# Layer 1's mixture of experts on pairs sorted by expert

## The chip, the cores and the metric

One Trainium2 chip; the kernel runs on one of its cores. The metric is the device time of one execution in microseconds, as the median over runs. A core has a matrix engine (TensorE, PE in the profile; its weight loads are PEld), VectorE (DVE), ScalarE (ACT), GpSimd (POOL) and SyncE (SP), each with its own queue that is worked off in order, and 16 DMA engines that all of them share.

## The reference

Two layers over `x` of 4 sequences, 1024 tokens, 128 features, all fp32. Each layer computes `x = x + s * silu(f)`, where `s` is an attention and `f` a mixture of experts, both of the layer-normed `x`. Layer 0 has 16 heads of 8 with relative positions, and one of 8 experts per token. Layer 1 has a causal differential attention (8 heads from 16 score maps, normed by head), and this mixture:

```python
logits = x @ router_w.T                       # T x 8
topk_logits, topk_idx = top_k(logits, 2)
probs = softmax(topk_logits)
combine[t, topk_idx] += probs                 # T x 8, two entries per row
hmid = gelu(einsum('th,efh->etf', x, w1) + b1)   # 8 experts, F = 256
y = einsum('etf,ehf->eth', hmid, w2) + b2
out = einsum('eth,te->th', y, combine)
```

Only two of the eight experts enter a token's result.

## The kernel before

Each layer and sequence is a `Sequence` `q` (`q.b` its number, `seqs` the eight in order: layer 0's four, then layer 1's four). Its attention is cut into steps (a group of 4 score maps, 256 queries) and these into slots, one block of 128 keys each: 128 slots for a sequence of layer 0, 80 for one of layer 1 (causal). `q.first` and `q.last` are its first slot and the slot after its last.

The order of all instructions is written out by hand. A loop goes over the slots; in each it issues the transposed scores (`turned_scores`, L912, into PSUM tag `st`, two buffers, exponentials on ACT at L950), half of the row-maximum searches (L793 scores, L853 maxima on DVE), the weighting of the slot before (`weigh`, L959), the other half, and then what `at(slot, f)` or, inside such work, `after(n, f)` has put there. `spread_over(lo, hi, work)` places work evenly over free slots. The searches of a step are done 7 slots or more before it in layer 1; the maxima go through `spread_maxima` and a store (`qs<-mt`) into the query tile. SP issues nearly all DMAs, in this written order: queries (`load_queries`, 10 slots before their first search), keys (`load_keys`), the splits of Q and K into bf16 pieces.

Around the change: `layernorm` makes `xn`, `transpose_xn` its transpose `xnT`; `values_of` also gives the router's logits; `route` finds the two largest of them, their softmax weights `p1`, `p2`, and the combine matrix `q.w`; `turn_route` and `expert_bias` start the gate's sum `q.g` with `b2`. Layer 1's experts are dense: for each half of the tokens and each of the 8 experts, `hidden` (L635, L643) makes 256 hidden values for 512 tokens with two 512-column matmuls and two Gelus, four experts in a row in one slot, and `experts1` (L655, L663, L670) multiplies back, weights by a column of `q.w` on DVE, and adds to `q.g` on POOL:

```python
for half in range(2):
    for e0 in range(0, NE, 4):
        some = range(e0, e0 + 4)
        work.append((lambda h=half, s=some: [hidden(q, h, e) for e in s], False))
        work += [(lambda h=half, e=e: experts1(q, h, e), True) for e in some]
```

The expert weights are transposed during layer 0 (`turn_expert`), stored to DRAM, and loaded at layer 1's first slot by `expert_tables` into the two `pos` tiles, which layer 0 needs no longer. `gate` applies tanh and two products to `q.g`; `norm_heads`, `turn_o` and `output` end a sequence.

## Time and profile before

| what | value |
|---|---|
| median of 3 runs | 2171.2 us (2167.64 to 2174.56) |
| the profiled execution | 2145.35 us, span 2143.6 us, granted clock 0.978 |
| layer 0, then layer 1 (first slot at about 1226 us) | 1226 us, 917 us |
| one sequence of layer 1 | 222 to 225 us |
| PE, DVE, ACT, POOL busy from 1226 to 2143 us | 839.07, 634.86, 430.26, 234.84 us |

The busy time of an engine is the time in which it worked on an instruction of the program; matmuls are pipelined, their ends are modelled, and a busy PE need not be at its peak. In the lists of groups a line names the source line, engine, operation, what is written and read, the shapes and the count; then come the busy time and the mean duration in ns, and after the second bar the engine's idle time just before these instructions and what ended it. The granted clock is the share of TensorE's full clock that the chip let through.

### The profile page before, as it was taken

The numbers are of one execution on the slowest core, as the hardware profiler recorded it, in microseconds if no ns is written. First come the engines' busy times: TensorE is split into PE (matmuls) and PEld (weight loads), VectorE is DVE, ScalarE is ACT, GpSimd is POOL, SyncE is SP. The second block draws the span as 40 slices with busy tenths as digits, with TensorE's granted clock in tenths as the row PEclk, the third lists the DMA queues.
The fourth block names the chain that finished last, engine by engine and source line by source line (L and its number), as shares of the span: only waits on it lengthen the run. The fifth ranks groups of instructions, "written<-read, shape, count | busy, mean of one in ns | idle before, by whom it ended". The sixth has DMA issues, their size and how long they took to land.

```text
span 2143.6 us, 45507 instructions
## 1 busy us (share of the span) xinstructions
PE 1969.8 (92%) x17424; PEld 1125.9 (53%) x17424; DVE 1613.7 (75%) x4197; ACT 1327.8 (62%) x1801; POOL 585.8 (27%) x907
## 2 busy tenths in 40 slices
PE   4899999999999999999999989999999899999996
PEld 2455555555555555555555445555556555555553
DVE  4788888787887888887888867778666876686563
ACT  1577778777778777886777544444555444544542
POOL 3013332224321333221323113313231324131112
PEclk9999999999999999998999989999999999999996
DMA  4766776767777767775767111201120212111001
GB/s 137 242 194 205 223 229 204 222 207 214 216 217 227 205 215 225 215 226 186 207 205 234 59 44 31 63 22 55 33 61 24 54 33 63 22 39 40 21 4 32
DMA packets 232975, 286.98 MB, mean 134 GB/s; under 512 B 14932, under 2 KB 206972, under 8 KB 232492
## 3 DMA queue, kind: packets, MB, share of 16 engines
q1 hardware_dynamic: 228272, 282.38, 44.1%
q8 instruction: 139, 2.28, 0.4%
q10 hardware_dynamic: 4476, 1.60, 0.3%
q14 instruction: 88, 0.72, 0.1%
HBM read 153.28 MB, written 129.76 MB: 132 GB/s over the span
## 4 chain that ended last, share of the span: by engine, by line
PE 63%; DVE 25%; DMA 7%; issue 3%; POOL 1%; SPq 1%; ACT 0%; DVEq 0%; ACTq 0%; POOLq 0%
PE s L793 14%; PE o L959 14%; DVE mx L853 7%; PE st L912 7%; PE st L944 6%; PE bank L655 6%; PE hid_ps L635 5%; DVE sp L809 4%; DMA qs<-qd 3%; DVE m L885 3%; DVE mx L828 2%; PE bank L600 2%; PE bank L716 2%; DVE mrest L887 2%; DMA skew<-rows 1%
## 5 line engine op out<-in xcount | busy, mean ns | idle before, releaser
L950 ACT ACTIVATE eT<-st 128x1024 f32<-128x1024 f32 x832 | 822.8, 991 | 561.5 <-PE st L912 515.7
L793 PE MATMUL s<-ksl,qs 72*128 72x384 bf16 (+3 forms) x1984 | 532.6, 312 | 64.1 <-DVE mx L853 35.9
L959 PE MATMUL o<-eT,va 128*9 128x256 f32 (+2 forms) x6656 | 520.8, 380 | 1.7 <-ACT eT L950 1.3
L853 DVE TENSOR_REDUCE mx<-s 128x1 f32<-128x512 f32 (+3 forms) x608 | 395.4, 657 | 55.3 <-PE s L832 26.4
L828 DVE TENSOR_REDUCE mx<-s 128x1 f32<-128x512 f32 x512 | 352.2, 688 | 106.6 <-PE s L793 101.1
L809 DVE CUSTOM_DVE_ANT_0 sp<-s,pos 128x512 f32<-128x512 f32 x512 | 352.2, 688 | 78.5 <-PE s L793 42.5
L793 PEld LDWEIGHTS <-qs 72*128 72x128 bf16 x2496 | 206.4, 98 | 382.7 <-issue 363.1
L878 ACT ACTIVATE sp<-sp,nm 128x384 f32<-128x384 f32 (+1 forms) x512 | 297.8, 583 | 107.7 <-DVE nm L870 107.7
L912 PE MATMUL st<-qs,ksl 75*128 75x256 bf16 (+1 forms) x2304 | 329.4, 253 | 0.0
L912 PEld LDWEIGHTS <-ksl 75*128 75x128 bf16 x2304 | 215.2, 99 | 70.6 <-issue 33.5
L944 PE MATMUL st<-ident,sp 128*128 128x128 f32 x1408 | 214.0, 277 | 0.2
L959 PEld LDWEIGHTS o<-eT,va 128*9 128x9 f32 (+1 forms) x6656 | 112.4, 91 | 182.5 <-issue 126.1
L732 POOL COPY rows<-rows 128x512 f32<-128x512 f32 x128 | 78.3, 612 | 428.5 <-ACT rows L723 391.7
L670 POOL TENSOR_TENSOR g<-g,part 128x512 f32<-128x512 f32 x64 | 81.2, 1269 | 402.8 <-DVE part L663 334.7
L944 PEld LDWEIGHTS st<-ident,sp 128*128 128x128 f32 x1408 | 172.6, 143 | 25.4 <-issue 15.5
L663 DVE TENSOR_TENSOR part<-bank,r1hot 128x512 f32<-128x512 f32 x64 | 44.2, 691 | 174.3 <-PE bank L655 159.8
L723 ACT COPY rows<-bank 128x512 f32<-128x512 f32 x256 | 147.8, 577 | 33.5 <-PE bank L716 22.2
L793 PE MATMUL s<-ksr,qs 72*128 72x128 bf16 (+3 forms) x512 | 157.3, 308 | 6.1 <-DVE mx L828 4.7
L655 PEld LDWEIGHTS bank<-pos,hid 128*128 128x128 f32 x1024 | 126.8, 198 | 15.3 <-issue 11.9
L655 PE MATMUL bank<-pos,hid 128*128 128x128 f32 x1024 | 131.2, 283 | 0.0
L716 PE MATMUL bank<-fs,qs 72*128 72x256 bf16 x512 | 101.2, 280 | 31.3 <-ACT rows L723 9.1
L912 PE MATMUL st<-qs,ksr 75*128 75x256 bf16 (+1 forms) x768 | 122.8, 260 | 0.0
(209 smaller groups left out, 2182.4 us busy)
## 6 DMA issues: line engine op xcount, KB each, us to landing
skew<-rows SPq DMA_DIRECT2D x128, 768.0 KB
pos<-skew SPq DMA_DIRECT2D x96, 768.0 KB
qs<-qd SPq DMA_DIRECT2D x384, 48.0 KB
ksl<-kd SPq DMA_DIRECT2D x96, 192.0 KB
pos<-skew SPq DMA_DIRECT2D x32, 512.0 KB
kd<-piece SPq DMA_DIRECT2D x36, 256.0 KB
ksr<-kd SPq DMA_DIRECT2D x48, 192.0 KB
qd<-piece SPq DMA_DIRECT2D x35, 256.0 KB
```

The lines of the kernel that those rows point to most:

```text
L655: nc.tensor.matmul(ps[:, m * P : (m + 1) * P], lhsT=h[:, c, m * P : (m + 1) * P], rhs=w2t[:, 2 * e + c, :], start=(c == 0), stop=(c == 1),)
L716: nc.tensor.matmul(ps[:, j * 256 : (j + 1) * 256], lhsT=st.qs[:NS, 2 * k + j, m * P : (m + 1) * P], rhs=fs, start=True, stop=True,)
L723: nc.scalar.copy(rows[:, 2 * k : 2 * k + 2, 0:256], ps.rearrange("p (m v) -> p m v", v=256))
L793: nc.tensor.matmul(ps, lhsT=st.qs[:NS, j, m * P : (m + 1) * P], rhs=keys[:NS, j, lo * P : hi * P], start=start, stop=stop,)
L809: nc.vector.tensor_tensor_reduce(out=st.sp[m][:, j * BW : j * BW + 512], in0=ps, in1=st.pos[m][:, j, :], scale=1.0, scalar=-FMAX, op0=ALU.add,
L828: nc.vector.tensor_reduce(largest(st)[:, m, j, 1:2], ps, AX.X, ALU.max)
L853: nc.vector.tensor_reduce(largest(st)[:, m, heads[0] : heads[-1] + 1, slot], parts, AX.X, ALU.max,)
L878: nc.scalar.activation(cols, cols, AF.Identity, bias=st.nm[:, m, j : j + 1])
L912: nc.tensor.matmul(ps[:, j, lo * P : hi * P], lhsT=keys[side][:, j, jb * P : (jb + 1) * P], rhs=st.qs[:, j, lo * P : hi * P], start=start, ...
L944: nc.tensor.transpose(ps[:, j, m * P : (m + 1) * P], st.sp[m][:, at : at + P], ident)
L950: nc.scalar.activation(eT[:, :, skip:], ps[:, :, skip:], AF.Exp)
L959: nc.tensor.matmul(o_ps[32 * j : 32 * j + va.shape[-1], skip : 2 * P], lhsT=va, rhs=eT[:, j, skip:], start=(jb == st.blocks[0]), stop=(jb ...
```

## The change

Each token of layer 1 makes two pairs (token, expert). The pairs are put in order of expert, each expert's padded to tiles of 128 rows: at most 23 tiles (`PT`) where the dense form has 64 products of 128 tokens with an expert. `pair_rows` counts with small matmuls and finds each pair's row and each tile's expert. `sort_tokens` scatters the normed tokens, read back from a DRAM copy (`xnd`), to their rows in `xsd`, 16 indirect DMAs of 128 rows from POOL's queue; `load_weights` gathers a tile's weights and bias, one indirect DMA a tile, from a table with 514 values a row; `load_pairs` and `turn_pairs` load and transpose four tiles; `hidden` and `results` work on four tiles, each with its own expert's weights, and the results go to `ysd`; `pick` gathers them back per token, 16 indirect DMAs, and DVE adds them to `q.g` with their weight. The weights and picks lie in the `pos` tiles and in the right-side key tiles, which layer 1 doesn't use. The next sequence's norm, values and routing are moved to earlier slots, and some steps of the norms a slot or more back. The output layout, layer 0's experts and the attention's arithmetic stay.

```diff
+PT = 2 * NT + NE - 1
+TRASH = PT * P
+WR = 4 * P + 2
...
+    onesb = const.tile([P, P], BF16, tag="onesb", name="onesb")
+    nc.gpsimd.memset(onesb, 1.0)
+    before = const.tile([P, P], BF16, tag="before", name="before")
+    up_to = const.tile([P, NE, NE], F32, tag="up_to", name="up_to")
...
-    w1d = dconst.tile([P, 2 * NE, P], F32, tag="w1d", name="w1d")
-    w2d = dconst.tile([P, 2 * NE, P], F32, tag="w2d", name="w2d")
+    wd = dconst.tile([NE * P, WR], F32, tag="wd", name="wd")
...
-            nc.sync.dma_start(w1d[:, 2 * e : 2 * e + 2, :], t[:, 0:2, :])
-            nc.sync.dma_start(w2d[:, 2 * e : 2 * e + 2, :], t[:, 2:4, :])
+            nc.sync.dma_start(wd[e * P : (e + 1) * P, : 4 * P], t.rearrange("p m f -> p (m f)"))
...
+    xnd = [dconst.tile([S, P], F32, tag=f"xnd{m}", name=f"xnd{m}") for m in range(2)]
+    xsd = [dconst.tile([TRASH + P, P], F32, tag=f"xsd{m}", name=f"xsd{m}") for m in range(2)]
+    ysd = [dconst.tile([TRASH + P, P], F32, tag=f"ysd{m}", name=f"ysd{m}") for m in range(2)]
+    spare = [t.rearrange("p h v -> p (h v)") for t in pos_tiles]
+    spare += [stacks[m][1].rearrange("p h t -> p (h t)").bitcast(F32) for m in range(2)]
+    weight_tiles = [t[:, m * WR : (m + 1) * WR] for m in range(3) for t in spare]
+    picked_tiles = [
+        t[:, 3 * WR + m * P : 3 * WR + (m + 1) * P] for m in range(3) for t in spare
+    ]
...
+    def zero_pairs():
+        zero = pos_tiles[0][:, 0:1, BW:].to_broadcast([P, PT + 1, P])
+        for t in xsd:
+            nc.scalar.dma_start(t.rearrange("(n p) d -> p n d", p=P), zero)
+        for t in ysd:
+            nc.scalar.dma_start(t[TRASH:], pos_tiles[0][:, 0, BW:])
...
-        after(1, guess)
-        after(2, refine)
+        after(2, guess)
+        after(3, refine)
...
-        after(10, lambda: nc.vector.tensor_tensor(xn, xn, over(rstd, full), ALU.mult))
+        after(11, lambda: nc.vector.tensor_tensor(xn, xn, over(rstd, full), ALU.mult))
+        if q.layer == 1:
+            q.xnd = xnd[q.b % 2].rearrange("(n p) d -> p n d", p=P)
+            after(12, lambda: nc.sync.dma_start(q.xnd, xn))
...
+                *pair_rows(q, hot1, hot2),
...
-            after(n, f)
+            after(n // 2 if q.layer else n, f)
...
+    def pair_rows(q, hot1, hot2):
+        ...
+        def counted():
+            ps = bank()
+            ahead.append(ps[:, : (NT + 1) * NE].rearrange("p (n e) -> p n e", e=NE))
+            nc.tensor.matmul(
+                ps[:, : (NT + 1) * NE],
+                lhsT=before,
+                rhs=both.rearrange("p n e -> p (n e)"),
+                start=True,
+                stop=False,
+            )
+            for n in range(NT):
+                nc.tensor.matmul(
+                    ahead[0][:, n + 1 :, :],
+                    lhsT=onesb,
+                    rhs=both[:, n : n + 1, :].to_broadcast([P, NT - n, NE]),
+                    start=False,
+                    stop=(n == NT - 1),
+                )
+            nc.vector.tensor_scalar(tiles, ahead[0][:, NT, :], P - 1.0, None, ALU.add)
+            nc.vector.tensor_copy(row, ahead[0][:, :NT, :])
+        many = [P, PT, NE]
+        work = [
+            lambda: nc.vector.memset(both[:, NT, :], 0.0),
+            lambda: nc.vector.tensor_tensor(both[:, :NT, :], hot1, hot2, ALU.add),
+            counted,
+            ...
+        for hot, rows in zip((hot1, hot2), q.rows):
+            work += [
+                lambda hot=hot: nc.vector.tensor_tensor(prod, hot, row, ALU.mult),
+                lambda: nc.vector.tensor_reduce(sums, prod, AX.X, ALU.add),
+                lambda rows=rows: nc.vector.tensor_scalar(
+                    rows, sums, float(TRASH), None, ALU.add
+                ),
+            ]
+        return work + [
+            lambda: nc.vector.tensor_tensor(
+                where,
+                tiles_at.unsqueeze(2).to_broadcast(many),
+                end.unsqueeze(1).to_broadcast(many),
+                ALU.is_ge,
+            ),
+            lambda: nc.vector.tensor_reduce(which, where, AX.X, ALU.add),
+            lambda: nc.vector.tensor_scalar(which, which, NE - 1.0, float(P), ALU.min, ALU.mult),
+            lambda: nc.vector.tensor_scalar(q.weight_rows, which, own_row, None, ALU.add),
+        ]
...
-    def expert_tables():
-        w1t = pos_tiles[0].rearrange("p h (c f) -> p (h c) f", f=P)
-        w2t = pos_tiles[1].rearrange("p h (c f) -> p (h c) f", f=P)
-        nc.sync.dma_start(w1t, w1d)
-        nc.sync.dma_start(w2t, w2d)
-        return w1t, w2t
-    def hidden(q, half, e):
-        w1t, _ = q.tables
-        ps = ps_t.tile([P, 2, 512], F32, tag="st", name="hid_ps")
-        h = four.tile([P, 2, 512], F32, tag="sp", name="hid")
-        for c in range(2):
+    def gather(dst, src, rows):
+        nc.gpsimd.indirect_dma_start(
+            out=dst,
+            out_offset=None,
+            in_=src,
+            in_offset=bass.IndirectOffsetOnAxis(ap=rows, axis=0),
+            bounds_check=src.shape[0] - 1,
+            oob_is_err=False,
+        )
+    def load_tokens(q, k):
+        q.again = one.tile([P, 4, P], F32, tag="wn", name="again")
+        nc.sync.dma_start(q.again, q.xnd[:, 4 * k : 4 * k + 4, :])
+    def sort_tokens(q, n, m):
+        to = xsd[q.b % 2]
+        nc.gpsimd.indirect_dma_start(
+            out=to,
+            out_offset=bass.IndirectOffsetOnAxis(ap=q.rows[m][:, n : n + 1], axis=0),
+            in_=q.again[:, n % 4, :],
+            in_offset=None,
+            bounds_check=to.shape[0] - 1,
+            oob_is_err=False,
+        )
+    def tiles_of(k):
+        return range(4 * k, min(4 * k + 4, PT))
+    def load_weights(q, n):
+        q.weights[n] = turn("weights", weight_tiles)
+        gather(q.weights[n], wd, q.weight_rows[:, n : n + 1])
+    def load_pairs(q, k):
+        q.pairs[k] = two.tile([P, 8, P], F32, tag="rows", name="pairs")
+        view = xsd[q.b % 2].rearrange("(n p) d -> p n d", p=P)
+        nc.sync.dma_start(q.pairs[k][:, 0:4, :], view[:, 4 * k : 4 * k + 4, :])
+    def turn_pairs(q, k):
+        t = q.pairs[k]
+        n = len(tiles_of(k))
+        transposed(t[:, 4 : 4 + n, :], [t[:, m, :] for m in range(n)])
+    def hidden(q, k):
+        x = q.pairs.pop(k)
+        ps = ps_t.tile([P, 4, 2, P], F32, tag="st", name="hid_ps")
+        q.hid[k] = h = four.tile([P, 4, 2, P], F32, tag="sp", name="hid")
+        both = [(m, n, c) for m, n in enumerate(tiles_of(k)) for c in range(2)]
+        for m, n, c in both:
             nc.tensor.matmul(
-                ps[:, c, :],
-                lhsT=w1t[:, 2 * e + c, :],
-                rhs=q.xnT[:, 4 * half : 4 * half + 4, :].rearrange("p n t -> p (n t)"),
+                ps[:, m, c, :],
+                lhsT=q.weights[n][:, c * P : (c + 1) * P],
+                rhs=x[:, 4 + m, :],
                 start=True,
                 stop=True,
             )
-        for c in range(2):
-            nc.scalar.activation(
-                h[:, c, :], ps[:, c, :], AF.Gelu, bias=b1t[:, 2 * e + c : 2 * e + c + 1]
-            )
-        q.hid[half, e] = h
-    def experts1(q, half, e):
-        _, w2t = q.tables
-        h = q.hid.pop((half, e))
+        for m, n, c in both:
+            bias = q.weights[n][:, 4 * P + c : 4 * P + c + 1]
+            nc.scalar.activation(h[:, m, c, :], ps[:, m, c, :], AF.Gelu, bias=bias)
+    def results(q, k):
+        h = q.hid.pop(k)
         ps = bank()
-        for m in range(4):
+        n = len(tiles_of(k))
+        for m, at in enumerate(tiles_of(k)):
             for c in range(2):
                 nc.tensor.matmul(
                     ps[:, m * P : (m + 1) * P],
-                    lhsT=h[:, c, m * P : (m + 1) * P],
-                    rhs=w2t[:, 2 * e + c, :],
+                    lhsT=h[:, m, c, :],
+                    rhs=q.weights[at][:, (2 + c) * P : (3 + c) * P],
                     start=(c == 0),
                     stop=(c == 1),
                 )
-        part = two.tile([P, 4, P], F32, tag="part", name="part")
-        nc.vector.tensor_tensor(
-            part,
-            ps.rearrange("p (m f) -> p m f", f=P),
-            q.w[:, 4 * half : 4 * half + 4, e : e + 1].to_broadcast([P, 4, P]),
-            ALU.mult,
-        )
-        acc = q.g[:, 4 * half : 4 * half + 4, :]
-        after(1, lambda: nc.gpsimd.tensor_tensor(acc, acc, part, ALU.add))
+        y = two.tile([P, 4, P], F32, tag="part", name="y_sb")
+        nc.vector.tensor_copy(y[:, :n, :], ps[:, : n * P].rearrange("p (m f) -> p m f", f=P))
+        view = ysd[q.b % 2].rearrange("(n p) d -> p n d", p=P)
+        after(1, lambda: nc.sync.dma_start(view[:, 4 * k : 4 * k + n, :], y[:, :n, :]))
+    def pick(q, n, m):
+        y = turn("picked", picked_tiles)
+        gather(y, ysd[q.b % 2], q.rows[m][:, n : n + 1])
+        p = (q.p1, q.p2)[m][:, n : n + 1]
+        g = q.g[:, n, :]
+        after(5, lambda: nc.vector.scalar_tensor_tensor(g, y, p, g, ALU.mult, ALU.add))
...
-        after(2, lambda: nc.vector.tensor_reduce(by_head[0], sq, AX.X, ALU.add))
-        after(3, lambda: inverse_root(rms, ms, 2 * HD, engine))
-        after(6, lambda: engine.tensor_scalar(rms, rms, 1.0 - LAMBDA_INIT, None, ALU.mult))
-        after(7, lambda: nc.vector.tensor_tensor(rows, rows, many, ALU.mult))
+        after(4, lambda: nc.vector.tensor_reduce(by_head[0], sq, AX.X, ALU.add))
+        after(5, lambda: inverse_root(rms, ms, 2 * HD, engine))
+        after(9, lambda: engine.tensor_scalar(rms, rms, 1.0 - LAMBDA_INIT, None, ALU.mult))
+        after(12, lambda: nc.vector.tensor_tensor(rows, rows, many, ALU.mult))
...
-        spread_over(q.last + (11 if q.layer else 9), q.last + (20 if q.layer else 28), tail)
+        spread_over(q.last + (16 if q.layer else 9), q.last + (25 if q.layer else 28), tail)
+    def sorted_experts(q):
+        first = q.first
+        for k in range(2):
+            at(first - 17 + 11 * k, lambda k=k: load_tokens(q, k))
+            for n in range(8):
+                slot = first - 14 + 11 * k + n
+                at(slot, lambda n=4 * k + n // 2, m=n % 2: sort_tokens(q, n, m))
+        for n in range(PT):
+            at(first + 4 + n + 10 * (n // 8), lambda n=n: load_weights(q, n))
+        places = []
+        for r in range(3):
+            start = first + 8 + 18 * r
+            pair = [k for k in (2 * r, 2 * r + 1)]
+            for m, k in enumerate(pair):
+                at(start + m, lambda k=k: load_pairs(q, k))
+            places += spread_over(
+                start + 4, start + 9, [(lambda k=k: turn_pairs(q, k), True) for k in pair]
+            )
+            at(start + 9, lambda pair=pair: [hidden(q, k) for k in pair])
+            spread_over(
+                start + 10, start + 17, [(lambda k=k: results(q, k), True) for k in pair]
+            )
+        for n in range(2 * NT):
+            at(first + 65 + n, lambda n=n: pick(q, n // 2, n % 2))
+        at(first + 65 + 2 * NT + 6, lambda: gate(q))
...
+                if seqs[k + 1].layer:
+                    spread_over(q.first + 54, q.first + 66, values)
                 spread_over(q.first + 76, q.first + 84, queries)
-                spread_over(q.first + 54, q.last - 24, values)
+                if not seqs[k + 1].layer:
+                    spread_over(q.first + 54, q.last - 24, values)
             else:
-                at(q.first + 6, work[0])
-                at(q.first + 13, work[1])
-                spread_over(q.first + 25, q.last - 30, turned + keys + queries + values)
+                at(q.first, work[0])
+                at(q.first + 6, work[1])
+                spread_over(q.first + 18, q.first + 44, turned + values + keys + queries)
         work = gates(q)
-        at(q.first - (24 if q.layer else 12) if k else 2, work[0][0])
-        end = q.last - 14 if q is seqs[-1] else q.last - 4
-        spread_over(q.first + (4 if k else 8), end, work[1:-1])
-        at(end + 7, work[-1][0])
+        if q.layer:
+            at(q.first - 40, work[0][0])
+            sorted_experts(q)
+            spread_over(q.first + 1, q.first + 20, work[1:-1])
+        else:
+            at(q.first - 12 if k else 2, work[0][0])
+            end = q.last - 4
+            spread_over(q.first + (4 if k else 8), end, work[1:-1])
+            at(end + 7, work[-1][0])
```

## The prediction

> **What bounds the kernel now.** I read the page's busy times first, then the windows over the second half, then the instruction groups from 1180 us on (layer 1), and last the timeline, the windows and the chain of waits around single places.
>
> ```profile
> PE 1969.8 (92%) x17424; PEld 1125.9 (53%) x17424; DVE 1613.7 (75%) x4197; ACT 1327.8 (62%) x1801; POOL 585.8 (27%) x907
> ```
>
> TensorE looks like the bound. Two windows of layer 1 say more: one whole sequence, and 56 us around its start in which no expert matmul runs. The columns are start:end, length, busy time (and count) of PE, PEld, DVE, ACT, POOL, then the granted clock, DMA share, GB/s.
>
> ```profile
> 1671.00:1894.00 223.00, 208.50 (x1842) 126.69 (x1834) 163.81 (x414) 107.60 (x126) 60.95 (x98) 0.98 0.16 42
> 1669.00:1725.00 56.00, 50.54 (x500) 28.95 (x503) 50.00 (x117) 24.65 (x27) 19.35 (x32) 0.97 0.20 53
> ```
>
> Over the sequence PE is busy 208.50/223 = 93%, DVE 73%. With the experts out of the way PE is at 0.903 and DVE at 50.00/56 = 0.893: both fill together, and PE waits for the row maxima. So VectorE is close behind, and a saving on PE counts only down to where DVE ends it. 26 slots in 56 us make a slot 2.15 us there.
>
> The groups that the change replaces, and rows that I price new work by (busy us and mean ns stand after the bar):
>
> ```profile
> L655 PE MATMUL bank<-pos,hid 128*128 128x128 f32 x1024 | 131.2, 283 | 0.0
> L635 PE MATMUL hid_ps<-xnT,pos 128*128 128x512 f32 x256 | 113.4, 596 | 0.0
> L670 POOL TENSOR_TENSOR g<-g,part 128x512 f32<-128x512 f32 x64 | 81.2, 1269 | 402.8 <-DVE part L663 334.7 <-DVE r2mx L535 32.8 <-DVE r1at L537 16.8
> L643 ACT ACTIVATE hid<-hid_ps,b1t 128x512 f32<-128x512 f32 x128 | 80.9, 683 | 32.5 <-PE hid_ps L635 32.5
> L663 DVE TENSOR_TENSOR part<-bank,r1hot 128x512 f32<-128x512 f32 x64 | 44.2, 691 | 174.3 <-PE bank L655 159.8 <-issue 12.7 <-PE st L912 1.5
> L643 ACT ACT_TABLE_LOAD x16 | 20.5, 1283 | 0.3
> L996 DVE TENSOR_TENSOR both<-turned,rinv 128x128 f32<-128x128 f32 x64 | 18.7, 292 | 3.5
> ```
>
> **PE, per sequence.** Removed: (131.2 + 113.4)/4 = 61.2 us. Added: 23 tiles with two hidden and two result matmuls each, all 128x128 fp32. 131.2 us over 512 such matmuls (two instructions each) is 0.256 us, so 92 x 0.256 = 23.6; 23 transposes at 0.15 (four take 0.59 us in the chain) = 3.4; nine small counting matmuls at 0.2 = 1.8. PE becomes 208.5 - 61.2 + 28.8 = 176.1; at the 0.903 of the expert-free window, 195.0 us.
>
> **DVE, per sequence.** Removed: 16 multiplications at 0.691 = 11.1. Added: 12 evictions of 128x512 (pairs turned, results) at 0.69 = 8.3; 16 picks at the 0.292 of L996 = 4.7; 21 small operations of `pair_rows` at 0.21 (the routing's 128x64 rows, as L537) = 4.4. DVE becomes 163.81 - 11.1 + 17.4 = 170.1; at 0.893, 190.5 us. PE's 195.0 is the larger, but only by 4: both engines will stand near 0.9.
>
> **ACT.** Gelu comes in three blocks a sequence instead of four, with 16 instructions of 128 columns. The 512-wide one takes 0.632 us by busy time; taking off 384 columns at 0.842 ns (the exponentials: 592 ns for 512, 1023 for 1024) leaves 0.31. A block runs 1.28 + 16 x 0.31 + 1.28 = 7.5 us. `ps_t` has two buffers and both hold hidden tiles, so the next slot's turned scores wait until half of it is done, 1.28 + 8 x 0.31 = 3.8 us, while PE has 16 instructions, 1.8 us, to run: 2 us of idle PE a block, 6 a sequence. Before, PE had 6.9 us of 512-column matmuls there. Sequence: 195 + 6 = 201 against 223, four times 22: **-88 us**.
>
> **The granted clock.** These idle spots have a second price. Timeline and windows around 1490 us:
>
> ```profile
> 1488.02 0.38 PE L793 MATMUL s<-ksl,qs 72*128 72x512 bf16 x1 [1.28 <-DVE mx L853]
> 1490.00:1493.40 3.40, 3.40 (x20) 2.14 (x19) 2.77 (x6) 1.02 (x1) 1.78 (x1) 0.50 0.10 29
> ```
>
> A gap of 1.28 us is followed by 3.4 us at half clock, up to 1.7 us lost. Twelve blocks: 0 to 20, I take **+10**. [...]
>
> **Start of layer 1.** The 2 MB of `expert_tables` go away. In the chain of waits they stand ahead of the first keys:
>
> ```profile
> 1228.91 9.51 DMA ksl<-kd
> ```
>
> **-5** (0 to -9.5).
>
> **The POOL queue.** POOL loses 20.3 us a sequence and gets 55 indirect DMAs (16 scatters, 23 weight gathers, 16 picks). No row shows one. Each scatter writes `xsd` after the one before it, so it waits for that one's landing: 16 run as a chain with period c = issue p + landing. For p I take 1.2 us: above SP's 0.37 for an issue, since POOL makes 128 row addresses, below the 2.36 of its costliest step, the 1024-wide product of `gate`; ends 0.4 and 2.4. For the landing of 64 KB, 2.0, below these stores of 256 KB in the chain (ends 0.4 and 2.8):
>
> ```profile
> 42.37 2.84 DMA kd<-piece
> 45.97 2.49 DMA kd<-piece
> ```
>
> So c = 3.2 (0.8 to 5.2). The chain starts at slot first-14 and its rows are transposed from first+12: 26 slots x 2.15 = 56 us, less two reads of 256 KB at about 3 us = 50, or c = 3.1. Until then `load_tokens` and `load_pairs` block SP's queue for some slots, but the maxima's stores behind them have 4 to 7 slots to spare, and queries are loaded 10 ahead. The weight gathers come 6 slots or more before their matmuls and are hidden. Picks alternate with the next sequence's scatters; at 3.2 us against a 2.15 us slot POOL falls 16 x 1.05 = 17 us behind over the 16 scatters, regains 2.9 in the three slots between their halves (6.5 less three picks), and DVE reads a pick 5 slots (10.8 us) after its issue, 7.6 after p and landing. What is left, 16 (c - 2.15) - 10.5 = 6 us, DVE waits at each of three sequence changes, and everything behind it in its queue, maxima first, waits too; at the first change, without picks, 16 (c - 3.1) = 2: **+20** (0 at the low end; 3 x 38 + 34 = 148 at c = 5.2). [...]
>
> **Ends.** In the tail the last gate moves from 7 slots before the last slot to 7 after it. Picks, tanh with its table and two products take some 10 us; the head norm that runs there now takes 13.7 us from the last sums to the first use of `g` (2118.9 to 2132.6). It covers most: **+3** (0 to 8). In layer 0, 3.1 MB of zeros are issued at about 18 us, when the windows show the DMA at 0.19 to 0.51 busy; 9 us at the 334 GB/s of the busiest window, mostly in free time: +3 (0 to 10). The first routing's 4.4 us of DVE add +2. The later `inverse_root` and norm slots are waits with slots to spare: 0.
>
> **Sum.** -88 + 10 - 5 + 20 + 3 + 5 = -55. The profiled execution took 2145.35 us (span 2143.6 and 1.75 around it), 1.2% under the median of 2171.2. 2090.35 there is 2171.2 x 2090.35/2145.35 = 2115.5: I say 2115.
>
> **Rivals.** *POOL's queue sets the pace.* By the two terms above the waits cost 64c - 184 us in all; at c = 4.05 they eat the 75 us that are left without them, and beyond that the kernel is slower. At c = 5.2: -75 + 148 = +73, about 2245. For it: 16 chained DMAs, POOL strictly in order, and `o_tok`, the norms and the splits behind them. Against: only 60.95 of 223 us of POOL are used. Chance 0.27. *No stall at all:* chain hidden, clock held: -88 - 5 + 3 + 2 = -88, 2082 and below, to 2055 if the engines reach 0.93. For it: the 26 slots of lead. Chance 0.20. *DVE stops at the 0.82 that layer 0 shows* (163.61 of 200 us from 600 to 800, with PE at 0.94): 170.1/0.82 = 207, plus 6, a saving of 40, and 28 of other costs leave about -10: 2160, in reach of no change. The expert-free window speaks against it. Chance 0.14, of which 0.04 is within 0.3% (what a measurement of this kernel can tell from no change). My forecast has 0.39.
>
> Faster: 0.39 + 0.20 + 0.10 = 0.69; same 0.04; slower 0.27. The range reaches to 2058, short of the best of the stall-free case, and to 2215, into the POOL rival up to c of about 4.7. The faster cases alone: 2058 to 2160.
>
> **What would show it.** Right: sequences of about 200 us, PE and DVE both near 0.9 between the blocks, 2 us of PE waiting for Gelu three times a sequence, scatters at about 3.2 us. Wrong: PE or DVE waiting for indirect DMAs for tens of us, a scatter period above 4 us, POOL busy most of a sequence, or granted clock well under 0.95 through layer 1.

## The result, and the profile after

The changed kernel took 2147.26 us (median), the kernel before 2164.47 in the same comparison: the ratio is **0.9934** (0.9906 to 0.9962), about 14 us faster. Ratios leave out executions in a slower state of the chip: one of the changed kernel's 20 here, at most one in the other sets, but six of the ten of the first run of experiment 6. The prediction had said 56 faster. The profiled execution took 2137.60 us (span 2135.8) against 2145.35 (2143.6); the readings below rest on these two traces. That of before is one of this kernel's fastest executions (the lowest is 2145.29), 19 us under its median; that of after is 10 us under its own. So the traces differ by 7.8 us and not by 14. One limit first: in two later comparisons, each on a chip of its own, the same changed kernel stood at 1.0241 and 1.0248 beside the kernel before. That slowdown is a matter of its own (experiment 6), and its traces are not mixed into the account of the 14 us.

The busy times and the granted clock on the page after:

```profile
PE 1904.9 (89%) x17008; PEld 1081.5 (51%) x17008; DVE 1664.9 (78%) x4329; ACT 1287.9 (60%) x1849; POOL 730.2 (34%) x1069
PEclk9999999999999999998999979896999989978996
```

PE lost only 64.9 us of busy time, although the change takes 4 x 32 us of work from it. The second line says why: in the second half, most of all in layer 1 (from the 24th slice of 53.4 us on), digits of 6 to 8 stand among the nines. PE does its smaller work in part at half speed. The four sequences of layer 1, with the columns that the prediction used (start:end, length, PE, PEld, DVE, ACT, POOL, clock, DMA share, GB/s):

```profile
1235.90:1463.90 228.00, 201.82 (x1745) 118.84 (x1745) 175.83 (x440) 98.03 (x139) 95.08 (x121) 0.86 0.34 93
1463.90:1680.80 216.90, 186.73 (x1744) 112.29 (x1743) 177.75 (x447) 98.07 (x139) 93.21 (x131) 0.93 0.35 97
1680.80:1914.00 233.20, 197.82 (x1745) 116.37 (x1745) 178.63 (x453) 97.98 (x138) 104.77 (x143) 0.88 0.34 94
1914.00:2097.10 183.10, 169.87 (x1625) 100.61 (x1623) 133.06 (x333) 94.92 (x132) 64.66 (x106) 0.93 0.30 83
```

Cut at the same places, the kernel before takes 230.8, 224.7, 224.6 and 214.1 us at clocks of 0.97, 0.98, 0.98 and 0.95. To separate work from clock I count, in windows where the clock was halved, half of PE's busy time as lost: the same instructions would have taken half as long (where 256-column matmuls of L1084 follow each other, they start 213 ns apart in such windows and 109 at full clock). This counts a little too much: the same kernel comes to 675.7 us of work with 80.7 lost here, and to 668.5 with 134.7 lost in experiment 6. With that, the time from the first exponential of layer 1 to the last falls into three parts (us):

| layer 1 | PE's work at full clock | PE idle | lost to half clock | length |
|---|---|---|---|---|
| before | 810.3 | 60.9 | 22.9 | 894.2 |
| after | 675.7 | 104.9 | 80.7 | 861.2 |
| difference | -134.6 | +44.0 | +57.8 | -33.0 |

Outside these sequences the time up to the kernel's first exponential grows by 3.4 us, layer 0 by 8.9, and what follows the last exponential by 12.9 (25.8 to 38.7). The sum is -7.8, the difference of the spans.

The groups of layer 1 that take the places of those shown before (busy us, mean ns, idle time before them and what ended it):

```profile
L773 POOL DMA_INDIRECT xsd<-again,rows x54 | 55.1, 1021 | 54.1 <-DMA xsd<-again,rows 48.9 <-issue 5.3
L757 POOL DMA_INDIRECT ksr<-wd,wrows x46 | 46.8, 1016 | 10.5 <-issue 6.3 <-PE s L1004 1.2 <-PE st L1084 0.8
L824 PE MATMUL bank<-pos,hid 128*128 128x128 f32 x184 | 27.7, 292 | 0.0
L824 PE MATMUL bank<-ksr,hid 128*128 128x128 f32 x184 | 27.3, 289 | 0.0
L806 PE MATMUL hid_ps<-pairs,pos 128*128 128x128 f32 x184 | 24.8, 275 | 0.0
L806 PE MATMUL hid_ps<-pairs,ksr 128*128 128x128 f32 x184 | 24.8, 275 | 0.0
L815 ACT ACTIVATE hid<-hid_ps,ksr 128x128 f32<-128x128 f32 x92 | 27.6, 413 | 7.3 <-PE hid_ps L806 7.3
L1057 DVE CAST m<-nm 128x8 bf16<-128x8 f32 x61 | 20.4, 335 | 2.1
```

Half of the tiles have their weights in `pos`, half in `ksr`, so the experts' matmuls have four rows here: they are down from 244.6 us to 104.6 (736 instructions, two for each of 368 matmuls). The chained scatters (L773) wait 48.9 us for one another, on POOL; experiment 6 found no time in it on the first chip that it ran on. The last row is a step that nobody priced: an 8-element cast whose mean is 335 ns here, though the median is 0.17 us.

What half clock looks like at its worst, at the end of sequence 0. Windows of 3.4 us, then the whole stretch, then the same at the end of sequence 2:

```profile
1439.90:1443.30 3.40, 2.09 (x20) 0.93 (x17) 3.23 (x12) 1.66 (x2) 2.70 (x3) 1.00 0.18 58
1443.30:1446.70 3.40, 3.06 (x20) 1.53 (x19) 2.51 (x8) 1.02 (x1) 2.48 (x4) 0.50 0.13 39
1450.10:1453.50 3.40, 3.40 (x20) 1.44 (x19) 1.71 (x5) 1.02 (x1) 2.55 (x3) 0.50 0.52 145
1463.80:1467.20 3.40, 3.40 (x29) 1.84 (x30) 2.41 (x6) 1.62 (x2) 1.01 (x1) 0.50 0.17 48
1443.30:1467.20 23.90, 23.56 (x144) 10.89 (x147) 15.25 (x38) 7.34 (x8) 16.14 (x18) 0.50 0.24 68
1893.90:1917.70 23.80, 23.80 (x148) 10.88 (x146) 15.09 (x38) 7.34 (x8) 16.39 (x18) 0.50 0.25 71
```

In the first window PE is busy for 2.09 of 3.4 us, with a gap of 0.56 us and one of 1.09 that begins in it. The clock then stays at 0.50 for seven windows, 24 us, although PE is busy for 23.56 of the 23.9 us. So this is no matter of idle time alone, and it does not end when the gap ends. Before, the drops between layer 1's first and last exponentials lasted 3.4 to 10.2 us.

**A rule that fits.** The clock in the records changes only on a fixed grid of 3.413 us. For each grid window I summed, over PE's matmul instructions, streamed columns (twice for fp32) x rows in use/128 x column groups of 32 in use/4, and divided by 4096 (256 columns every 213 ns make about 4100 in a window at half clock). Where the sum is below about 0.725 the next window is at half clock, and above it at full clock, whichever clock the window itself had. From about 100 us on this holds for 588 of 596 windows after (some 70 of them are at half clock) and, at 0.72, for 595 of 599 before (some 20); busy time alone, or columns without the weights, misses more than 30 after. In the first 100 us it does not hold: 24 windows after and 22 before have smaller sums, down to 0.05, and full clock follows. At half clock these windows of pure attention stay under the mark: the seven above come to .63, .62, .67, .69, .72, .71 and .71. The last is one of the rule's misses, since full clock followed it. Windows with expert matmuls (128 rows) for most of their length come to 0.8 and more even then. The rule was found by fitting; experiments 1 and 3 test it.

In the trace of after, several drops followed windows whose longest gap was 0.95 to 1.3 us, and stayed through windows without a gap (0.95 before the drops at 1893.9 and 1934.8, which lasted 24 and 20.5 us; 1.03 before 1006.4, 10 us).

### The profile page after: what moved, and what is told of

Read it like the earlier page. It is cut to its first block, busy times and chain, and to the rows that moved or that the text cites. A ratio compares the mean times of both kernels' runs of the same rounds, so it can differ in the third digit from the quotient of the medians.

```text
span 2135.8 us, 45469 instructions
## 1 busy us (share of the span) xinstructions
PE 1904.9 (89%) x17008; PEld 1081.5 (51%) x17008; DVE 1664.9 (78%) x4329; ACT 1287.9 (60%) x1849; POOL 730.2 (34%) x1069
## 3 DMA queue, kind: packets, MB, share of 16 engines
q8 instruction: 135, 2.21, 0.4%
## 4 chain that ended last, share of the span: by engine, by line
PE 58%; DVE 26%; DMA 5%; issue 4%; ACT 3%; POOL 3%; SPq 0%; DVEq 0%; POOLq 0%; ACTq 0%
PE s L965 15%; PE o L1131 14%; PE st L1084 7%; PE st L1116 7%; DVE mx L1025 6%; DVE sp L981 4%; DVE m L1057 3%; DVE mx L1000 2%; PE bank L824 2%; DVE mrest L1059 2%; PE bank L734 2%; PE bank L888 2%; ACT hid L815 2%; DMA qs<-qd 2%; PE s L1004 1%
## 5 line engine op out<-in xcount | busy, mean ns | idle before, releaser
L965 PE MATMUL s<-ksl,qs 72*128 72x384 bf16 (+3 forms) x1984 | 550.9, 321 | 92.7 <-DVE mx L1025 64.4
L1131 PE MATMUL o<-eT,va 128*9 128x256 f32 (+2 forms) x6656 | 535.3, 389 | 8.1 <-ACT eT L1122 7.7
L965 PEld LDWEIGHTS <-qs 72*128 72x128 bf16 x2496 | 210.7, 100 | 397.1 <-issue 379.2
L1084 PE MATMUL st<-qs,ksl 75*128 75x256 bf16 (+1 forms) x2304 | 346.1, 262 | 7.5 <-ACT hid L815 7.5
L1084 PEld LDWEIGHTS <-ksl 75*128 75x128 bf16 x2304 | 222.7, 103 | 97.5 <-issue 62.5
L1116 PEld LDWEIGHTS st<-ident,sp 128*128 128x128 f32 x1408 | 175.1, 145 | 25.5 <-issue 15.3
L1178 POOL TENSOR_TENSOR o_tok<-both 128x32 f32<-128x32 f32 x128 | 30.2, 258 | 289.7 <-DVE both L1168 289.2
L1084 PE MATMUL st<-qs,ksr 75*128 75x256 bf16 (+1 forms) x768 | 124.3, 262 | 0.0
L888 PE MATMUL bank<-fs,qs 72*128 72x256 bf16 x512 | 101.6, 281 | 23.9 <-ACT rows L895 7.3
L750 POOL TENSOR_TENSOR part<-part 128x256 f32<-128x256 f32 x64 | 46.6, 729 | 217.6 <-DVE part L742 207.1
L1004 PE MATMUL s<-mask_q,identb 128*128 128x128 bf16 (+1 forms) x416 | 102.0, 251 | 0.0
L1004 PEld LDWEIGHTS <-identb 128*128 128x128 bf16 x672 | 69.5, 103 | 58.9 <-issue 53.2
```

Of the source, the lines that this page charges most:

```text
L888: nc.tensor.matmul(ps[:, j * 256 : (j + 1) * 256], lhsT=st.qs[:NS, 2 * k + j, m * P : (m + 1) * P], rhs=fs, start=True, stop=True,)
L965: nc.tensor.matmul(ps, lhsT=st.qs[:NS, j, m * P : (m + 1) * P], rhs=keys[:NS, j, lo * P : hi * P], start=start, stop=stop,)
L1004: nc.tensor.matmul(ps, lhsT=identb, rhs=mask.unsqueeze(1).to_broadcast([P, ps.shape[1], P]), start=opens, stop=not opens,)
L1084: nc.tensor.matmul(ps[:, j, lo * P : hi * P], lhsT=keys[side][:NR, j, jb * P : (jb + 1) * P], rhs=st.qs[:, j, lo * P : hi * P], start=star ...
L1116: nc.tensor.transpose(ps[:, j, m * P : (m + 1) * P], st.sp[m][:, at : at + P], ident)
L1131: nc.tensor.matmul(o_ps[32 * j : 32 * j + va.shape[-1], skip : 2 * P], lhsT=va, rhs=eT[:, j, skip:], start=(jb == st.blocks[0]), stop=(jb ...
```

## The experiments

### 1. Turned scores with 128 rows instead of 75

If rows in use count, then keys and queries padded with zero rows (K = 75 to 128) cost PE no columns and should hold the clock. The same edit was made on both kernels. The zero rows come by DMA, at the start.

```diff
+        rows = P if q.layer else NR
-                lhsT=keys[side][:NR, j, jb * P : (jb + 1) * P],
-                rhs=st.qs[:, j, lo * P : hi * P],
+                lhsT=keys[side][:rows, j, jb * P : (jb + 1) * P],
+                rhs=st.qs[:rows, j, lo * P : hi * P],
...
-        st.qs = six.tile([NR, HG, 2 * P], BF16, tag="qs", name="qs")
+        st.qs = turn("qs", q_tiles)
```

On the changed kernel:

> The changed kernel; in layer 1 the turned scores (L1084) contract over 128 rows instead of 75. Rows 75 to 127 of the key stacks and of the six query tiles are zeroed once at the start, so the sums and the number of streamed columns stay the same. Clock theory: the profile of the changed kernel spends 261 us at half clock (96 before), and in both traces a grid window of 3.41 us is followed by half clock when its matmuls, each counted as streamed columns x rows in use / 128 x column groups of 32 in use / 4, fill less than about 0.73 of what the half clock could stream. Layer 1's attention alone reaches only 0.6 to 0.74 at half clock, so a drop holds itself up to 24 us; the experts' 128x512 matmuls, now gone from the ends of a sequence, used to end it. With 128 rows the mix lies above the bound: half-clock time falls to 150 us or less and the time by 30 to 50 us against the changed kernel (about 2100 to 2115). Rival (VectorE late behind GpSimd's new instructions sets the pace, clock a mere echo): the waits for maxima stay, less than 5 us gained.

On the kernel before:

> The kernel before with the same edit, the turned scores of layer 1 over 128 rows. Clock theory: here the experts' dense matmuls already end each drop after one to three windows, so little is to be had: half-clock time from 96 to about 70 us, time 2 to 8 us lower. If the extra rows helped by something else than the clock's recovery, both kernels would gain alike.

The totals came out at 1.0158 (1.0078 to 1.0238) and 1.0237 (1.0185 to 1.0288), because the DMAs that bring the zeros delayed the first exponential by 64 and 66 us (80.7 to 144.8; 77.3 to 143.1). Within layer 1 the half-clock loss fell from 80.7 to 45.7 us and from 22.9 to 6.8; the length fell by 11.6 and by 10.0, since idle time grew by 18.7 and 5.4 (11.0 of the 18.7 are new waits for the queries' DMA, which the fixed tiles bring). The rows count, zeros or not. As an improvement it failed: only a third of the 35.0 us of clock that came back on the changed kernel became time.

### 2. The last weight gathers moved out of slots 40 to 48

In these slots three sequences each show one wait of 4.06 us at PE. The timeline around the first (start, us, engine, line; idle time and its releaser in brackets):

```profile
1350.75 2.65 DVE L1057 CAST m<-nm 128x8 bf16<-128x8 f32 x1
1351.22 2.14 POOL L575 TENSOR_TENSOR rest<-rest,piece 128x1024 f32<-128x1024 f32 x1
...
1353.84 1.77 DVE L1059 TENSOR_TENSOR mrest<-mrest,m 128x8 f32<-128x8 f32 x1
...
1354.52 1.05 POOL L564 CAST piece<-rest 128x1024 bf16<-128x1024 f32 x1
...
1357.06 0.48 PE L965 MATMUL s<-ksl,qs 72*128 72x384 bf16 x1 [4.06 <-DVE mx L1025]
```

DVE's cast of 8 elements ends at 1353.40, with POOL's long product at 1353.36; its next product ends at 1355.61, with POOL's cast at 1355.57. DVE ends with POOL both times, so I read it as held while POOL works, and the maxima that PE waits for stand behind it in DVE's queue. The edit moves gathers 16 to 22 to other slots, so that POOL's gathers and its splits no longer meet.

```diff
-            at(first + 4 + n + 10 * (n // 8), lambda n=n: load_weights(q, n))
+            slot = 4 + n + 10 * (n // 8)
+            if n >= 16:
+                slot = 14 + n if n < 20 else 27 + n
+            at(first + slot, lambda n=n: load_weights(q, n))
```

> The changed kernel; the last seven weight gathers of a sequence are issued at slots first+30 to 33 and first+47 to 49 instead of first+40 to 46, away from the splits on GpSimd. Contention theory (a small VectorE copy waits for GpSimd's back-to-back instructions: L1057 2.65 us and L1059 1.77 us around 1351 us, and TensorE then waits 4.06 us): the three waits of 4.06 us vanish and with them the half clock that follows, 10 to 18 us. If GpSimd's instructions were the main cause of the missing 42 us, more than 25. If the splits alone block VectorE, nothing.

Measured 0.9885 (0.9851 to 0.9919). The 4.06-us waits became 2.4 to 2.6 us; over three sequences the slots 40 to 48 went from 88.8 us to 73.8, with idle time from 25.9 to 13.5. The means of the cast `m<-nm` and of the product `mrest<-mrest,m` fell from 335 and 332 ns to 259 and 252. So the meeting with POOL cost 15.0 us in these slots; over the whole of layer 1 the trace is 8.4 us shorter (861.2 to 852.8). The interval overlaps that of the changed kernel (0.9906 to 0.9962), which did not run beside it, so the total alone doesn't prove the gain; the slots do show it.

### 3. Less expert work at the edges of the kernel before

The theory says that dense expert matmuls held the clock up, and that taking them out is what costs. Here the kernel before keeps all its work, but its hidden and result matmuls leave the slots 0 to 16 and 62 to 80 of each sequence.

```diff
-        spread_over(q.first + (4 if k else 8), end, work[1:-1])
+        if q.layer:
+            spread_over(q.first + 1, q.first + 10, work[1:5])
+            spread_over(q.first + 17, q.first + 62, work[5:-1])
+        else:
+            spread_over(q.first + (4 if k else 8), end, work[1:-1])
```

> The kernel before with all its experts; in layer 1 their matmuls are spread over slots first+17 to first+62 instead of first+4 to last-4, so that the 128x512 matmuls no longer stand in the last 18 and first 17 slots of a sequence, as in the changed kernel. No work is added or taken. Clock theory: at these ends nothing dense follows a drop any more; the half-clock loss of slots 72 to 80 and 0 to 16 of the first three sequences rises from 6 us to 25 or more and the time by 10 to 25 us. If the drops come from the new GpSimd and VectorE instructions, the loss at the ends stays near 6, since none of those is here; the middle may still be a little slower for being fuller.

Measured 1.0103 (1.0067 to 1.0139). Layer 1 grew by 20.0 us (894.2 to 914.2): the loss from 22.9 to 37.0, idle time from 60.9 to 68.1. The new loss lies in slots 0 to 16 (17.1 us over the first three sequences, 6.2 before); slots 72 to 80 of these lost nothing, so that 17 came where 25 or more had been expected. So the mechanism is there without any sorting, gather or pick, but thinning alone does not make a drop everywhere: at full clock a window of attention without a gap counts about 1.2, as the two before the stretch above do (1.16 and 1.21), so it takes a gap as well. The same kernel was then run beside one in which zero rows fill the turned scores to 128 (here by a `memset` at the start, with a seventh query tile and one buffer fewer for the key splits; the bias matmul's weights are filled to 128 rows too):

```diff
+        nc.gpsimd.memset(t.rearrange("p h t -> p (h t)").bitcast(F32)[64:], 0.0)
...
-                lhsT=q.wT[:, n * P : (n + 1) * P],
+                lhsT=q.wT[: P if q.layer else NE, n * P : (n + 1) * P],
```

> before_squeezed unaltered, as the control of this call: about 1.010 of the kernel before, half-clock loss of layer 1 about 37 us against 23.

> before_squeezed with the 128 rows of the kernel rows (turned scores and gate bias of layer 1 over zero rows), and nothing of the sorted experts: no scatters, picks or gathers. Clock theory: the squeezing cost time because no dense matmul ends a drop at the ends of a sequence; with 128 rows the attention's own matmuls end it. The half-clock loss of layer 1 falls from 37 to 15 us or less and the time by 10 to 20 us, though the zero rows cost some 4 us at the start: back to 1.000 to 1.006. If the squeezing costs by the fuller middle instead, the ratio stays at 1.010 or rises.

Without the rows 1.0098 (1.0064 to 1.0132), with them **0.9962** (0.9935 to 0.9989): 2176.29 and 2146.82 us. In layer 1 the loss fell from 38.6 to 3.4 us (-35.2), idle time hardly moved (65.9 to 65.3), and the length fell by 33.7: lost clock turned into time one to one. Slots 8 to 16 of sequence 1, without the rows:

```profile
1485.00:1507.60 22.60, 21.36 (x157) 10.81 (x155) 18.19 (x42) 7.74 (x8) 5.95 (x19) 0.72 0.17 57
```

and with them:

```profile
1478.20:1497.80 19.60, 15.97 (x157) 8.95 (x155) 18.38 (x45) 7.74 (x8) 5.96 (x19) 1.00 0.20 68
```

The same 157 matmul instructions take 21.36 us at a clock of 0.72 and 15.97 at 1.00. Gaps like the two that ended in a drop of 10.2 us just before these slots (0.63 and 0.76 us) are still there (0.73 and 0.76). In sequences 1 and 3 their windows now come to 0.77 and more, and nothing drops; in sequence 2 one comes to 0.71, and the drop after it lasts a single window (over the whole run the rule misses at most three windows). Note that PE is "busy" 95% of the first of these two stretches and 81% of the second, and the second is the faster. This version also beats the kernel before, by 9 us between the medians (2155.77 to 2146.82).

### 4. The 128 rows on the changed kernel

The same edit on the changed kernel, alone and with the moved gathers and the tail edit of experiment 5:

> As k128_after, but the zero rows are written by memsets in the idle start, a seventh query tile takes away the wait for queries that the fixed tiles brought, and the gates' bias product of layer 1 (L720, 8 rows) contracts over 128 rows too, 120 of them zero. Sums and streamed columns are unchanged. Ledger of layer 1 in the changed kernel: TensorE's work at full clock 676 us, idle 105, half-clock loss 81; k128_after had 46 of loss and 124 idle, 11 of it for queries. Clock theory: the loss falls to 25 to 40 (slots 8 to 16, where L720 runs, from 24 to under 12 over three sequences), no start cost, so 20 to 45 us below the changed kernel, about 2100 to 2125. If VectorE takes back what the clock gives, idle rises as much as the loss falls and less than 8 us is gained.

> rows, with the last seven weight gathers moved as in gathers_moved and, in the last sequence alone, the picks issued two to a slot from slot 64 and the gate ten slots earlier, ahead of the last step's subtraction. If the three causes (clock held down, VectorE blocked at the splits, the last gate in the tail) add up: 25 for the first, 10 for the second, 12 for the third, so about 2095 to 2105, ratio to before 0.970 to 0.978. If VectorE ends every stage anyway, only the tail's 12 on top of gathers_moved: 0.982.

1.0143 (1.0101 to 1.0185) and 1.0181 (1.0148 to 1.0214), where a gain was hoped for. Both ran on another chip than experiments 1 and 2, so the same kernels were run again beside the unedited one:

> The kernel of rows, beside the changed kernel. Clock theory: 20 to 45 us below it less what VectorE takes back; the first profile of rows had 53 us of half-clock loss in layer 1 against 81 and about 25 us of unexplained standstill. Without that standstill the two must differ by the 28 us less the growth of idle time, so 10 to 20 us. If restoring the clock is worth nothing, they are equal.

> rows_moved_tail again, beside the changed kernel: the sum of the two above, 30 to 45 us below the changed kernel if the three causes are independent; equal to moved_tail if VectorE takes back what the clock gives.

1.0122 (1.0061 to 1.0183) and 1.0151 (1.0083 to 1.0220), with the unedited kernel at 1.0241 on that chip (experiment 6). Beside it the rows gain 18.6 us in the medians (2207.55 to 2188.94). In layer 1 the loss fell from 134.7 to 57.2 us, but idle time grew from 129.8 to 164.5, so that the length fell by 33.5; 4.8 us were given back before the first exponential and 13.4 in layer 0. Their intervals touch (1.0172 to 1.0310; 1.0061 to 1.0183), with four executions each. On the squeezed kernel before, the edit kept all it gained; on the changed kernel waits take the place of the slow clock. Most of them are waits for VectorE: in layer 1 PE's waits for the maxima (`mx`) before its searches went from 64.6 us to 94.8, those for `os` from 9.9 to 16.5. What keeps VectorE is not shown.

### 5. An earlier tail

The chain of waits after the last slot, from the last picks on (start, us, engine, line):

```profile
2105.34 1.00 POOL ksr L757
2106.33 0.30 issue
2106.64 2.63 DMA ksr<-ysd,rows
2109.31 0.04 issue
2109.36 0.35 DVE g L842
...
2111.11 2.21 DVE newton L441
2113.34 0.19 DVE newton L442
2113.55 2.21 DVE newton L443
...
2118.09 0.44 DVE o_tok L1199
```

The end waits for the last pick's landing. Then two steps of the norm take 2.21 us instead of 0.19, while POOL runs the gate's two 1024-wide products (2110.93 to 2115.73): 4.0 us more, as in experiment 2. The edit picks two rows a slot from slot 64 on in the last sequence, and gates ten slots sooner.

```diff
-            at(first + 65 + n, lambda n=n: pick(q, n // 2, n % 2))
-        at(first + 65 + 2 * NT + 6, lambda: gate(q))
+            slot = 64 + n // 2 if q is seqs[-1] else 65 + n
+            at(first + slot, lambda n=n: pick(q, n // 2, n % 2))
+        at(first + (77 if q is seqs[-1] else 87), lambda: gate(q))
```

> The changed kernel; in the last sequence the 16 picks are issued two to a slot from slot 64 and the gate at slot 77 instead of 87; nothing else. The tail after the last exponential takes 38.7 us in the changed kernel and 25.8 before. If picks and gate in front of the last subtraction and norm on GpSimd make the difference, the tail falls to 25 to 28 and the time by 10 to 13 us. If the half clock of the tail makes it, nothing changes.

> The changed kernel with the moved weight gathers and the early picks and gate of the last sequence together, without the 128 rows. The tail after the last exponential was 26.1 us with the early picks against 38.7, and gathers_moved stood about 10 us under the changed kernel: 20 to 25 us below it, about 0.982 of the kernel before where the standstill does not occur.

> The changed kernel with the moved weight gathers and the early picks and gate of the last sequence. 10 us for the three waits of 4 us and 12 for the tail: 18 to 25 us below the control of this call.

The tail alone did what it should to the tail, 38.7 to 26.1 us after the last exponential, but the kernel stood at 1.0266 (1.0221 to 1.0311), with no unedited one beside it. With the moved gathers it was 1.0198 (1.0112 to 1.0283) beside 1.0241 for the unedited kernel, and in the repeat 1.0259 (1.0215 to 1.0303) beside 1.0248. There the last sequence took 213 us with the early picks, against 183.5 without, and lost 37.5 us to half clock against 5.2; in the comparison before it took 202.6 against 200.3. Whether two picks a slot do this is not shown. No gain. The moved gathers, too, no longer show: slots 40 to 48 still fell from 89.6 us to 73.8, but 24 to 32 rose from 60.0 to 72.2.

### 6. POOL's chain, and the slower chips

The prediction's largest unknown was the chain of scatters and picks on POOL. This kernel leaves out the scatters and the gathers of the picks (the picks' multiplications stay, on a tile's old contents):

```diff
-                at(slot, lambda n=4 * k + n // 2, m=n % 2: sort_tokens(q, n, m))
+                pass
...
-        y = turn("picked", picked_tiles)
-        gather(y, ysd[q.b % 2], q.rows[m][:, n : n + 1])
+        y = picked_tiles[n % 2]
```

> The changed kernel without its 64 scatters and 64 picks: the pairs are zeros and a fixed stretch of SBUF is added per token; weight gathers, matmuls and VectorE's 64 additions stay. The prediction's term for the scatter chain and the picks was +20 us. If GpSimd's queue costs that, the time falls by 20 us or more. Clock theory: the drops around the sequence changes come from ordinary waits for maxima and last because no dense matmul follows, so 0 to 10 us.

0.9922 (0.9873 to 0.9971), the changed kernel's 0.9934 again; over all its ten executions the median is 2158.67 us, the kernel before's 2158.63. So no gain shows from leaving the chain out, though the changed kernel itself did not run beside it. In the changed kernel's profile the scatters follow each other every 2.5 us where nothing stands between (1249.24, 1251.75, 1254.26; 2.7 us is the median of all), with 1.02 us to issue one; 3.2 and 1.2 had been assumed.

The controls on two more chips:

> The changed kernel unaltered, to stand beside the other three on one chip. In the profiles of rows, rows_moved_tail and tail the engines stand still for 20 to 25 us over the first three sequences in slots 64 to 72, with nothing in the profile that releases them; in those of the changed kernel, k128_after, gathers_moved and no_chain, taken elsewhere, they do not. If the chip makes that difference, this copy shows it too where the others do; if the edits make it, this copy stays near 0.993.

> The changed kernel unaltered, as the control of this call. It measured 0.993 of the kernel before in its first comparison and 1.024 in a later one on another chip; the 60 us between them lie in slots 64 to 80 of layer 1, where scatters and picks alternate. Here it gives either about 2145 or about 2205.

1.0241 (1.0172 to 1.0310) and 1.0248 (1.0184 to 1.0312): 49 and 53 us slower than the kernel before, which kept its time on every chip (medians of 2156 to 2159 there). In the first of them layer 1 took 933.0 us, with 134.7 lost to half clock and 129.8 idle. With the second ran two kernels that leave out half of the chain each, first the picks' gathers, then the scatters:

> The changed kernel without the 64 gathers of the picks; VectorE adds a fixed stretch of SBUF in their place, all else stays. If the picks' landings cause the standstill of slots 64 to 80, and this chip shows it, 50 to 60 us below the control; if the scatters do, no more than 10. If the control shows none, 0 to 10 below it: the prediction's stall on picks would then be nothing on either side.

> The changed kernel without its 64 scatters; the pairs stay zero, all else stays. The prediction's scatter chain held 2 us at the first sequence change and, with the picks, 6 at each of the others. If the chain sets a wait, 10 to 20 us below the control; with a period of 2.5 us as the profile shows, instead of 3.2, it is hidden and nothing changes. If the scatters cause the standstill, 50 to 60 us.

Without the picks' gathers 1.0064 (1.0034 to 1.0093), 39 us less than the control's 2208.71; without the scatters 1.0193 (1.0151 to 1.0236), 11 less; with four executions each and intervals that overlap, these 11 are neither shown nor excluded as a wait for the chain. The picks' gathers are not all of the slowdown: without them the trace still loses 107.9 us to half clock in layer 1, where the first one lost 80.7, and 1.0064 stands above 0.9934. Slots 64 to 72, the first with picks, went from 24.9 us of idle PE to 2.0. The timeline of the control among the first picks:

```profile
1428.07 1.00 POOL L757 DMA_INDIRECT pos<-ysd,rows  x1 [0.31 <-issue]
...
1431.67 0.69 DVE L1025 TENSOR_REDUCE mx<-s 128x4 f32<-128x512 f32 x1 [2.54 <-PE s L1004]
...
1433.87 0.42 DVE L1142 COPY os<-o 128x256 f32<-128x256 f32 x1 [1.51 <-remote]
...
1434.35 0.44 PE L1150 MATMUL turned<-ident,os 128*128 128x128 f32 x2 [3.18 <-issue]
...
1435.34 1.02 ACT L1122 ACTIVATE eT<-st 128x1024 f32<-128x1024 f32 x1 [4.00 <-PE turned L1150]
```

PE, DVE and ACT all stand for 1.5 to 4 us within 5 us, and the releasers shown ("remote", "issue", a matmul that ended earlier) are no running work. These places appear on three chips, with the first picks of each sequence, and vanish with the picks' gathers. Neither the first comparison nor experiments 1 and 2 show them. What holds the engines is open: no row names it, and since each chip was used in one comparison, no run separates the chip's part from that of the occasion. For a program that must run on any chip, the gain of 0.66% is therefore not to be relied on.

## Why the prediction was wrong, point by point

Most signs were right. One size was far off, and its place too.

| step | predicted | measured |
|---|---|---|
| PE's work less, with the waits around it | -88 | -90.6 (-134.6 + 44.0) |
| granted clock in layer 1 | +10 | **+57.8** |
| start of layer 1, zeros and routing in layer 0 | -5 + 5 | +12.3 |
| scatters and picks on POOL | +20 | no time found |
| tail | +3 | +12.9 |
| sum | -55 | -7.6 |

**PE's work.** Four times 32.4 = 129.6 us were taken off; 134.6 went. That is close by luck: groups overlap in the trace, and both sides were priced too high. Taken out of the traces, the old experts' matmuls free 216.8 us of PE at full clock (244.6 had been counted), and the new ones with their transposes and counts 86.5 (4 x 28.8 = 115.2 counted). A 128x128 matmul has 104.6/368 = 0.284 us of busy time, and not 0.256. Idle time was to grow by 4 x (201 - 176.1) - 4 x (223 - 208.5) = 41.6; it grew by 44.0. Part of that agreement is luck too. The waits at the Gelu blocks are there (idle time in slots 16 to 24, 32 to 40 and 48 to 56 of three sequences: 9.1 to 29.6 us, +20.5 where 18 were predicted). Of it, 12.1 us are waits that end with ScalarE (5.7 for a Gelu, 6.4 for an exponential behind it), 1.3 us a block instead of 2, and a Gelu tile takes 27.6/92 = 0.30 us (0.31 predicted). But 17.5 us more come from slots 40 to 48, where DVE is held by POOL (experiment 2), which was in no term.

**The clock: the step that failed.** "A gap of 1.28 us is followed by 3.4 us at half clock, up to 1.7 us lost. Twelve blocks: 0 to 20, I take +10." The row was read rightly. Wrong was to price a drop at one window, and to look for drops at the Gelu blocks alone. In layer 1 the slots of the blocks (16 to 24, 32 to 40, 48 to 56) lost 5.5 us over the four sequences, against 6.6 before; slots 8 to 16 lost 34.4 (5.1 before), slots 72 to 80 20.2 (5.0) and slots 40 to 48 14.3 (3.4). Before, the dense fp32 matmuls of the experts kept the count up, and no drop between the sequences' first and last exponentials outlasted 10.2 us. The change takes away more than half of these (244.6 to 104.6 us), so a drop now lasts up to 24 us, and gaps of about 1 us (0.95 before the drops at 1893.9 and 1934.8) began some outside the Gelu blocks too. PE's work was counted as time to be saved, when it was also what kept the clock. The prediction's own sign of being wrong, a clock well under 0.95 through layer 1, came: 0.86 to 0.93. Experiment 3 shows the size by itself: 35.2 us less loss, 33.7 us less time. Experiment 1 lowered the loss of both kernels by the same edit. What is not shown is that the changed kernel would have run the 57.8 us faster with the clock held: of the clock that the rows gave back there, a third (experiment 1) and two fifths (experiment 4, 33.5 of 77.5 us) became time. Waits took the rest.

**POOL's chain.** The period came out at 2.5 to 2.7 us, below the 3.1 at which it begins to cost, and leaving the chain out showed no gain on the first chip. The rival built on it (2245) fell with its price; what the later chips show at the picks is something else, since the scatters' period there is the same 2.7 us.

**No stall at all** needed a clock that holds: 0.86 to 0.93 in place of 0.98. **DVE stopping at 0.82** came nearest in time (2160 us), and sequence 1 even shows 177.75/216.9 = 0.82. But its mechanism isn't what set the clock loss: in the two windows of experiment 3, DVE's share goes from 18.19/22.60 = 0.80 to 18.38/19.60 = 0.94 when hardly more than the clock changes: there DVE was waiting for a slow PE. In the changed kernel itself VectorE may be the next limit, since the waits that took the place of the slow clock in experiment 4 are mostly for its maxima.

**Start and layer 0.** Nil was predicted, +12.3 came in these traces: 3.4 us before the first exponential and 8.9 in layer 0 (1146.4 to 1155.2), where the half-clock loss also doubled, from 11.7 to 23.6. The 8.9 can't be put down to the zeros or the routing: the squeezed kernels of experiment 3 leave layer 0 as it was and took 1161.2 and 1158.6 us for it, with 25.5 and 22.0 lost. The wait for the first keys behind the tables' 2 MB, 3.1 us of idle PE before, is gone, and stands in the idle time above.

**Tail.** The cover failed: +3 was taken in a range of 0 to 8. The picks' landing ends late and the norm, which was to hide it, comes after it, and is itself held for 4.0 us by the gate's products.

## What to carry to other kernels

Before taking matmuls out of a TensorE-bound stage, look at what is left there: if its instructions use few rows or column groups, as this attention's do, the clock may no longer hold, and the saving shrinks by what that slows of the rest (here 57.8 us beside 134.6 of work taken off). Price a clock drop by what follows the gap, not by one window, and judge PE by work at full clock: "busy 100%" at a clock of 0.50 is a loss that no wait shows. Work given to an idle POOL cost DVE time here where the two met (15.0 us over slots 40 to 48 of three sequences; the gate's products cost the last norm 4.0), so place gathers away from splits and norms.

## What the runs showed of the hardware

- From about 100 us on, the granted clock of 588 of 596 windows follows a count of columns weighted by rows and column groups in use, on a grid of 3.413 us with a mark near 0.725. Zero rows count like others (loss 38.6 to 3.4 us in experiment 3). A drop after gaps of 0.56 and 0.95 us lasted 24 us with PE busy throughout (1893.9 to 1917.7).
- 8-element DVE instructions with a median of 0.17 us took up to 2.65 us, and the longest ended with a POOL instruction: DVE at 1353.40, POOL at 1353.36.
- An indirect DMA of 128 rows took POOL 1.02 us to issue. The last pick landed 2.63 us after its issue began, and dependent scatters followed each other at 2.5 to 2.7 us.
- In some comparisons, waits of 1.5 to 4 us on three engines at once go with the row gathers of the picks: 24.9 us of idle PE in slots 64 to 72 with them, 2.0 without. The cause is open.
